# Seven block products in the second product of a mixture of experts, with scatters and searches reordered

## The chip, the cores and the metric

The kernel runs on one core of a Trainium2 chip. The metric is the device time of one execution in microseconds, given as the median over runs; the profile shows one further execution. Engines: PE is TensorE (matmuls; PEld its weight loads), DVE is VectorE, ACT is ScalarE, POOL is GpSimd, SP is the engine that issues most plain DMAs.

## The reference

The program is a stack of four sublayers over tokens of width 256 (4 x 1024 rows): a gated attention, a low-rank feed-forward, a ReLU attention with 16 heads, and a mixture of experts in which each expert chooses its tokens. Each is wrapped as `x = x + layernorm(sublayer(layernorm(x)))`. The change touches only the last one:

```python
def _L1_ffn_ref(x, Wg, W1, b1, W2, b2):
    b, l, h = x.shape                    # 4096 tokens in all, h = 256
    e = Wg.shape[1]                      # 8 experts
    n = b * l
    k = min(max(int(n * 2 / e), 1), n)   # 1024 tokens an expert
    xt = x.reshape(n, h)
    S = jax.nn.sigmoid(xt @ Wg).T
    G, I = jax.lax.top_k(S, k)           # each expert takes its best 1024
    ex = xt[I]
    hid = jax.nn.gelu(jnp.einsum('ekh,ehf->ekf', ex, W1) + b1[:, None, :], approximate=False)   # f = 1024
    out = (jnp.einsum('ekf,efh->ekh', hid, W2) + b2[:, None, :]) * G[..., None]
    new_x = jnp.zeros_like(xt).at[I.reshape(-1)].add(out.reshape(-1, h))
    return new_x.reshape(b, l, h)
```

Everything is float32.

## The kernel before

**The stages.** The first 950 us or so are the three sublayers ahead. From there on the mixture of experts runs, expert after expert. An expert's 1024 chosen tokens are eight chunks of 128; four chunks are a unit, so expert e has the units u = 2e and 2e + 1 (`QPE` is 2, `NJ` is 4 chunks a unit, `TB` is 512 tokens).

**Choosing.** A `Search` (line 1806) finds the 1024th largest score of one or more experts, three bits at a time in ten ticks: VectorE compares and counts, TensorE adds the counts over partitions with one small matmul, VectorE keeps the best candidate. A `List` (line 1891) then turns a threshold into indices: sort, rank, chunks, places, collect, gather. The last step issues eight indirect DMAs on GpSimd's queue that fetch the tokens (`got`). Before the change the searches are for expert 0, for 1, for 2 and 3, and for 4 to 7. Expert 0's search and list run ahead of everything. All other steps stand in one list, `agenda`, and are taken from its head: `go_on_with_lists(u, time)` (line 2357) is called between matmul groups, subtracts `time` from a budget `left`, and runs the next step once the budget is used up and unit u is late enough for it. The first three steps of the second search run while expert 0's tokens are on their way.

**The first product.** `turn` transposes the tokens on TensorE into `xT`. Experts 0, 1, 2 and 7 go through `feed_forward` (line 2275), unit by unit: for each of eight slices f of the hidden width two matmuls with 512 columns, and a gelu on ScalarE into `hid`. Experts 3 to 6 go through `feed_forward_by_seven` (line 2225): both units are handled together as a 2 x 2 block product, with seven block products in place of eight (Strassen's scheme in Winograd's form). The sums of blocks of the weights are made by GpSimd (`weight_sums`), those of the tokens by VectorE (`token_sums`), and the products are combined by VectorE.

**The second product.** `project_back(u, hid)` (line 2307) does one unit. For each of its four chunks, eight matmuls with 256 columns accumulate over the hidden width; VectorE adds the bias and multiplies by the gate; GpSimd issues an indirect DMA that adds the 128 rows to `acc_d` in DRAM (line 2333). The scatters of an expert are ordered among themselves, but for those of expert 6. Between chunks the tokens of the next unit are turned (`turns_within`).

**The last expert.** Expert 7 doesn't scatter. When all scatters of expert 6 have landed (`summed`), `begin_last` reads the accumulator back in blocks of 512 tokens (`read_back`) and fetches expert 7's own rows of it (`fetch_acc`). The table `beside_last` (line 2134) writes out by hand what is done after which matmul group of units 14 and 15: the statistics of a block (`all_stats`, VectorE and GpSimd), its scaling (`all_scaled`, ScalarE), its store (`all_out`), and the same for expert 7's own rows (`chosen_...`).

**What sets the order.** In this stage TensorE, VectorE and ScalarE execute in the order of the program. GpSimd's and SP's order is found by the scheduler, and from expert 6 on GpSimd's too is that of the program. PSUM has five banks tagged `mm` and two tiles tagged `y`.

Of the kernel before, what the change touches and what calls it, by code (L numbers as in the profile page):

```python
# [9 lines left out]
F32 = mybir.dt.float32  # L10
# [4 lines left out]
ALU = mybir.AluOpType  # L15
# [59 lines left out]
def kernel(  # L75
# [1679 lines left out]
    with ExitStack() as st4:  # L1755
# [135 lines left out]
        class List:  # L1891
# [59 lines left out]
            def steps(self):  # L1951

                behind = max(QPE * self.e - 3, 0)
                return [
                    (0.5, behind, self.sort),
                    (2.6, behind, self.rank),
                    (1.2, behind, self.chunks),
                    (1.4, behind, lambda: (self.places(0), self.places(1))),
                    (1.4, behind, lambda: (self.places(2), self.places(3))),
                    (0.3, behind, lambda: [self.collect(part) for part in range(4)]),  # L1960

                    (0.3, behind + 1, self.gather),
                ]
# [62 lines left out]
        summed, stores, replaced, room_back, ys, chosen = [], [], [], [], {}, {}  # L2026
        last = lists[NE - 1]

        def after_all(one, others):
# [90 lines left out]
        def begin_last():  # L2120
# [13 lines left out]
        beside_last = {  # L2134
            (0, "f", 5): [(all_stats, 0)],
            (0, "f", 6): [(all_stats, 1)],
            (0, "f", 7): [(all_scaled, 0), (known, 0), (all_stats, 2), (fetch_acc, 4, 5)],
            (0, "i", 0): [(all_out, 0), (all_scaled, 1), (known, 1), (all_stats, 3)],
            (0, "i", 1): [(all_out, 1), (all_scaled, 2), (known, 2), (all_stats, 4), (fetch_acc, 6, 7)],
            (0, "i", 2): [(all_out, 2), (all_scaled, 3), (known, 3)],  # L2140
            (0, "i", 3): [(all_out, 3), (all_scaled, 4), (all_stats, 5)],
            (1, "f", 0): [(all_out, 4)],
            (1, "f", 1): [(all_scaled, 5, front), (all_stats, 6)],
# [22 lines left out]

        def turn(u, c, half=None):

            if c == 0 and not half:
                xT[u] = wk.tile([P, DC, TB], F32, tag="xT", name="xT")  # L2170
            e, q = divmod(u, QPE)
            tiles = range(NJ) if half is None else range(half * NJ // 2, (half + 1) * NJ // 2)
            tp = ps.tile([P, NJ, P], F32, tag="mm", name="tp", bufs=5)
            for i in tiles:
                nc.tensor.transpose(tp[:, i, :], lists[e].got[q * NJ + i][:, c * P : (c + 1) * P], ident)
                if u == 0 and c == 0 and i == 0:

                    keep_busy(first, 4)
            cols = slice(tiles[0] * P, (tiles[-1] + 1) * P)
            copy = nc.scalar.copy if by_seven(e) else nc.vector.tensor_copy  # L2180
            copy(xT[u][:, c, cols], tp.rearrange("p j t -> p (j t)")[:, cols])  # L2181

        def by_seven(e):

            return 3 <= e < NE - 1

        rooms = [x.rearrange("p j d -> p (j d)")[:, h * TB : (h + 1) * TB] for x in xs[:4] for h in range(2)]
# [21 lines left out]
        def turns_within(u):  # L2209

            e, q = divmod(u, QPE)
            if u == QPE * NE - 1:
                return {}
            turns = {c: (lambda c=c: turn(u + 1, c)) for c in range(DC)}
            if q == QPE - 1 and by_seven(e + 1):
                both = [
                    turns[0], turns[1], lambda: turn(u + 2, 0), lambda: token_sums(e + 1, 0), lambda: turn(u + 2, 1),
                    *(lambda n=n: token_sums(e + 1, n) for n in (1, 2, 3)),
                ]
                return {0: both[0:1], 1: both[1:4], 2: both[4:]}  # L2220
            if by_seven(e) and q == 0:
                return {}
            return {2: [turns[0], turns[1]]} if u == 1 else {1: [turns[0]], 2: [turns[1]]}

        def feed_forward_by_seven(e):
# [14 lines left out]
            def gelu(n, f, src):  # L2240
                gelus.append(nc.scalar.activation(hid[n][:, f, :], src, AF.Gelu, bias=mb1[:, e * FC + f : e * FC + f + 1]))

            HC = FC // 2
            for f in range(HC):
# [20 lines left out]
                nc.vector.tensor_tensor(c12, u2, d, ALU.add)  # L2265
                gelu(1, f, c12)
                go_on_with_lists(QPE * e, 3.0)
            for q in range(QPE):
                if q == 0 and by_seven(e + 1):
                    weight_sums(e + 1, gelus[-1])  # L2270
                if q == 0 and e == NE - 2:
                    fetch_last()
                project_back(QPE * e + q, hid[q])

        def feed_forward(u):
            e, q = divmod(u, QPE)
            w1, w2 = weights[e]
            hid = wk.tile([P, FC, TB], F32, tag="hid", name="hid")

            n = TB if u else TB // 2  # L2280
            for h in range(TB // n):
# [3 lines left out]
                for f in range(FC):  # L2285
# [14 lines left out]
                    if u or h or f not in (FC - 5, FC - 4, FC - 3):  # L2300
                        go_on_with_lists(u, 1.75 if u else 0.87)
                    aside(u, "f", f)
            if q == QPE - 1 and by_seven(e + 1):
                weight_sums(e + 1, gelu)
            project_back(u, hid)

        def project_back(u, hid):
# [4 lines left out]
            for i in range(NJ):  # L2312
                k = q * NJ + i
                py = ps.tile([P, D], F32, tag="y", name="py")
                for f in range(FC):
                    nc.tensor.matmul(  # L2316
                        py,
                        lhsT=hid[:, f, i * P : (i + 1) * P],
                        rhs=w2[:, f, :],
                        start=(f == 0),  # L2320
                        stop=(f == FC - 1),
                    )
                for do in ahead.get(i, ()):
                    do()
                gates = lists[e].got[k][:, D + e : D + e + 1]
                if e == NE - 1:
                    nc.vector.scalar_tensor_tensor(accg[:, k, :], py, gates, accg[:, k, :], ALU.mult, ALU.add)
                    aside(u, "i", i)
                    continue
                y = wk.tile([P, D], F32, tag="y", name="y", bufs=7)  # L2330
                nc.vector.tensor_tensor(y, py, mb2[:, e, :], ALU.add)  # L2331
# [9 lines left out]
                )  # L2341
                if e == NE - 2:

                    beside_each_other(scatter, summed)
                go_on_with_lists(u, 3.4 if by_seven(e) else 2.3)

        searches = [Search(0), Search(1), Search(2, 3), Search(4, 5, 6, 7)]
        agenda = []  # L2350
        for search in searches[1:]:
            agenda.extend(search.steps())
            for e in search.es:
                agenda.extend(lists[e].steps())
        left = [0.0]

        def go_on_with_lists(u, time, within=False):
            left[0] = max(left[0] - time, 0.0)
            if agenda and left[0] < 0.3 and agenda[0][1] <= u and not (within and agenda[0][0] not in (0.5, 1.2, 1.4)):
                spent, _, step = agenda.pop(0)  # L2360
                left[0] += spent
                step()

# [16 lines left out]
        for _ in range(3):  # L2380
            agenda.pop(0)[2]()
            keep_busy(first, 4)
# [51 lines left out]
```

## Time and profile before

| what | us |
| --- | --- |
| median of 3 runs | 1458.32 (1456.48 to 1459.18) |
| the profiled execution, its own time | 1456.37 |
| its span | 1454.2 |
| expert 0, from its first product | 988.68 to 1049.30 |
| expert 1 | 1049.30 to 1108.41 |
| expert 2 | 1108.41 to 1169.19 |
| expert 3 | 1169.19 to 1224.23 |
| expert 4 | 1224.23 to 1279.29 |
| expert 5 | 1279.29 to 1334.33 |
| expert 6 | 1334.33 to 1388.20 |
| expert 7 and the close | 1388.20 to 1454.2 |

The borders of the experts are the starts of their first matmul. In a row of groups the columns are: source line, engine, operation, the tiles that it writes and reads, the shape, the count, then the busy time of the group and the mean duration of one in ns. In a row of the timeline they are: start in us, duration in us of a merged run, engine, line, operation, tiles, count, and in brackets how long the engine stood idle before and what ended that. A row of the table by stage has, for each engine, its busy microseconds and instruction count in that stretch, then the granted TensorE clock (1.00 is full), the busy share of the DMA engines, and GB/s.

### The profile page before, as it was taken

Reading aid. Unit: us, or ns where it says so; the run is one execution under the profiler, and the core shown is the slowest. Engines: PE = TensorE matmul, PEld = TensorE weight load, DVE = VectorE, ACT = ScalarE, POOL = GpSimd, SP = SyncE. Lnnn points to the kernel's source line nnn. Section 1 sums busy time; section 2 is a strip of 40 time slices with the busy share of each in tenths; the row PEclk is TensorE's granted clock in tenths of the full one; section 3 lists DMA queues with packets and bytes.
Section 4 is the critical chain, followed back from the end, with each engine's and each line's share of the span. In section 5 each row is a group of like instructions: output and inputs, shape, how many; then the busy total and the mean of one; then the engine's idle time right before and its main releaser. Section 6 shows DMA issues by size and latency. Waiting matters only on the chain.

```text
span 1454.2 us, 26447 instructions
## 1 busy us (share of the span) xinstructions
PE 1405.7 (97%) x10392; PEld 858.6 (59%) x10392; DVE 869.7 (60%) x2133; ACT 735.8 (51%) x1014; POOL 531.7 (37%) x662
## 2 busy tenths in 40 slices
PE   8999999999889999999999999949999999999997
PEld 4666666666644444454444547727666657757774
DVE  5457555666554637664767496885545766365346
ACT  4244454454358887877787888712122131231243
POOL 4123322322352223422333323413425325543765
PEclk9999999999999999999999999979999999999999
DMA  8400000001652473437344721151414233343364
GB/s 223 142 1 1 0 1 1 1 1 38 203 173 76 122 209 104 143 118 232 91 133 144 229 70 39 39 170 38 106 19 127 51 79 70 78 103 62 81 166 134
DMA packets 104853, 138.76 MB, mean 95 GB/s; under 512 B 25469, under 2 KB 64794, under 8 KB 104602
## 3 DMA queue, kind: packets, MB, share of 16 engines
q1 hardware_dynamic: 74512, 81.75, 18.1%
q0 software_dynamic: 30160, 55.32, 16.1%
q8 instruction: 81, 1.33, 0.4%
q14 instruction: 42, 0.34, 0.1%
q10 hardware_dynamic: 58, 0.01, 0.0%
HBM read 75.29 MB, written 61.51 MB: 94 GB/s over the span
## 4 chain that ended last, share of the span: by engine, by line
PE 87%; DVE 5%; issue 3%; POOL 2%; DMA 1%; ACT 1%; SPq 0%; POOLq 0%; ACTq 0%; DVEq 0%
PE po L1553 16%; PE py L2316 14%; PE sc L1532 10%; PE ph L2290 7%; PE ph L2236 7%; PE pg L722 4%; PE pv L738 4%; PE py L848 3%; PE pt L1308 2%; PE pq L397 2%; PE po L820 2%; PE ph L904 2%; PE pv L431 2%; PE po L824 1%; PE pkv L835 1%
## 5 line engine op out<-in xcount | busy, mean ns | idle before, releaser
L1710 ACT ACTIVATE w<-sc 128x1024 f32<-128x1024 f32 x395 | 379.9, 1023 | 60.7 <-PE sc L1532 60.2
L1553 PE MATMUL po<-w,vaug 128*17 128x256 f32 (+1 forms) x4608 | 256.0, 358 | 1.5 <-DVE turned L1611 1.2
L2316 PE MATMUL py<-w,hid 128*128 128x256 f32 x1024 | 228.6, 380 | 0.0
L2316 PEld LDWEIGHTS py<-w,hid 128*128 128x128 f32 x1024 | 191.9, 190 | 29.6 <-issue 4.2
L1712 DVE TENSOR_SCALAR w<-sc 128x1024 f32<-128x1024 f32 x117 | 142.4, 1220 | 79.4 <-PE sc L1532 75.9
L1553 PEld LDWEIGHTS po<-w,vaug 128*17 128x17 f32 x4608 | 116.3, 97 | 117.9 <-issue 48.2
L1532 PE MATMUL sc<-q,kT 64*128 64x512 f32 (+1 forms) x1152 | 170.3, 403 | 2.5 <-ACT w L1710 1.3
L2333 POOL DMA_INDIRECT acc_d<-y,idx x56 | 88.6, 1583 | 163.0 <-issue 38.6
L1532 PEld LDWEIGHTS sc<-q,kT 64*128 64x128 f32 x1152 | 90.1, 185 | 83.5 <-issue 46.6
L2297 ACT ACTIVATE hid<-ph,mb 128x512 f32<-128x512 f32 (+1 forms) x72 | 46.0, 639 | 159.6 <-PE ph L2290 133.3
L2290 PE MATMUL ph<-xT,w 128*128 128x512 f32 (+1 forms) x288 | 114.8, 552 | 0.3 <-DVE xT L2181 0.3
L2005 POOL DMA_INDIRECT got<-tok_d,idx x64 | 66.6, 1040 | 72.1 <-DVE idx L1995 54.1
L2290 PEld LDWEIGHTS ph<-xT,w 128*128 128x128 f32 x288 | 52.6, 190 | 51.3 <-issue 48.3
L371 POOL DMA_DIRECT2D kT<-k_d x32 | 23.4, 732 | 118.0 <-PE sc L1532 54.0
L722 PE MATMUL pg<-nT,wh 128*128 128x512 f32 x128 | 61.6, 613 | 1.5 <-ACT nT L661 1.5
L2331 DVE TENSOR_TENSOR y<-py,mb 128x256 f32<-128x256 f32 x56 | 23.5, 420 | 64.3 <-PE py L2316 54.9
L848 PE MATMUL py<-wo,oT 128*128 128x256 f32 x256 | 61.6, 384 | 0.0
L738 PE MATMUL pv<-wh,nT 128*128 128x512 f32 x128 | 59.7, 593 | 0.0
L848 PEld LDWEIGHTS py<-wo,oT 128*128 128x128 f32 x256 | 47.5, 190 | 17.6 <-issue 11.1
L746 ACT ACTIVATE v<-v 128x512 f32<-128x512 f32 x32 | 20.2, 630 | 62.7 <-DVE v L745 62.7
L1137 POOL TENSOR_TENSOR rsb<-veb,mhalf 128x1 f32<-128x1 f32 x30 | 19.6, 654 | 86.8 <-DVE veb L1136 86.8
L586 POOL TENSOR_TENSOR x<-x,y 128x1024 f32<-128x1024 f32 x13 | 30.6, 2357 | 56.3 <-ACT y L575 56.3
(352 smaller groups left out, 2344.8 us busy)
## 6 DMA issues: line engine op xcount, KB each, us to landing
q<-q_d POOLq DMA_DIRECT2D x16, 1024.0 KB, 6.0
kT<-k_d POOLq DMA_DIRECT2D x32, 512.0 KB, 8.1
w<-in_L_ffn_W_dram SPq DMA_DIRECT2D x16, 1024.0 KB
k_d<-parts SPq DMA_DIRECT2D x48, 256.0 KB
q_d<-parts SPq DMA_DIRECT2D x48, 256.0 KB
acc_d<-logits SPq DMA_DIRECT2D x8, 512.0 KB
tok_d<-hg SPq DMA_DIRECT2D x30, 128.0 KB
x<-in_L_attn_x_dram SPq DMA_DIRECT2D x7, 512.0 KB
```

What stands on the lines that cost most here:

```text
L722: nc.tensor.matmul(pg, lhsT=wh[:, c, HID + e * P : HID + (e + 1) * P], rhs=d["nT"][:, c, :], start=(c == 0), stop=(c == DC - 1),)
L738: nc.tensor.matmul(pv, lhsT=d["nT"][:, c, i * P : (i + 1) * P], rhs=wh[:, c, 0:HID], start=(c == 0), stop=(c == DC - 1),)
L848: nc.tensor.matmul(py, lhsT=d["oT"][:, e, :], rhs=wo[:, e, :], start=(e == 0), stop=(e == EC - 1))
L1532: nc.tensor.matmul(sc[:, j, m * n : (m + 1) * n], lhsT=row["kT"][t, r][rows, u, (kt + m) * P : (kt + m + 1) * P], rhs=row["q"][qh, t][rows ...
L1553: nc.tensor.matmul(po[rows : rows + HD + 1, at : at + n], lhsT=row["v"][:, kt + m, HQ * t + 4 * r + 2 * u + j, :], rhs=w[:, j, (2 * m + pa ...
L1710: nc.scalar.activation(w, sc, AF.Relu)
L1712: nc.vector.tensor_scalar(w, sc, 0.0, None, ALU.max)
L2005: return nc.gpsimd.indirect_dma_start(out=dst, out_offset=None, in_=rows[:, :], in_offset=self.at_chunk(c), bounds_check=NT - 1, oob_is_er ...
L2236: nc.tensor.matmul(bank, lhsT=a[:, f * P : (f + 1) * P], rhs=b, start=start, stop=stop, skip_group_check=not start)
L2290: nc.tensor.matmul(ph, lhsT=w1[:, c, f * P : (f + 1) * P], rhs=xT[u][:, c, h * n : (h + 1) * n], start=(c == 0), stop=(c == DC - 1),)
L2316: nc.tensor.matmul(py, lhsT=hid[:, f, i * P : (i + 1) * P], rhs=w2[:, f, :], start=(f == 0), stop=(f == FC - 1),)
L2333: scatter = nc.gpsimd.indirect_dma_start(out=acc_d[:, :], out_offset=lists[e].at_chunk(k), in_=y, in_offset=None, bounds_check=NT - 1, oob ...
```

## The change

The second product of experts 1 to 6 is done by a new function, `project_back_by_seven`, for both units of an expert at once. The hidden values are a 2 x 2 block matrix (512 tokens by 512 hidden), W2 is one (512 hidden by 128 columns), and seven block products take the place of eight. A block product is 16 accumulating matmuls of 128 columns. GpSimd makes the sums of W2's blocks (`back_sums`) into the rooms of the attention weights, which are no longer needed; VectorE makes the sums of the hidden blocks, combines the products and adds them, multiplied by the gate, to a tile that ScalarE has filled with bias times gate. All eight scatters of an expert come in two groups: four after the seventh product, four after the last. Experts 1 and 2 keep their first product; their second unit's tokens are now turned within the first unit. Tokens of the experts 1 to 6 are copied out of PSUM by ScalarE, and turned in the `y` banks.

Scatters of one expert are declared independent; each waits for those of the expert before. The searches are for 0, for 1 to 3, and for 4 to 7; the last two have an agenda each, and a step of the second is taken where the head of the first isn't due yet. The sort of a list may begin one unit earlier. Budgets of some calls change, and in the table for the last expert the block statistics come one step later.

```diff
+        def back_sums(e, behind):
+            (b11, b12), (b21, b22) = back_blocks(e)
+            t1, t2, t4 = (room.rearrange("p (f n) -> p f n", n=P) for room in back_rooms[:3])
+            for dst, x, y in ((t1, b12, b11), (t2, b22, t1), (b12, b22, b12), (t4, b21, t2)):
+                after_all(nc.gpsimd.tensor_tensor(dst, x, y, ALU.subtract), [behind])
...
+            def product(bank, a, b, start, stop):
+                for i in range(NJ):
+                    if i == NJ // 2:
+                        lists_too(0)
+                    for f in range(HC):
+                        nc.tensor.matmul(
+                            bank[:, i * P : (i + 1) * P],
+                            lhsT=a[:, f, i * P : (i + 1) * P],
+                            rhs=b[:, f, :],
...
+            def of_bias(q):
+                for k in range(q * NJ, (q + 1) * NJ):
+                    ys[k] = wk.tile([P, D], F32, tag="y", name="y", bufs=9)
+                    nc.scalar.activation(ys[k], mb2[:, e, :], AF.Identity, scale=gates[k])
...
+            p1 = new_bank("p1")
+            product(p1, a11, b11, True, True)
+            nc.scalar.copy(u2, p1)
+            nc.vector.tensor_tensor(s1, a21, a22, plus)
+            nc.vector.tensor_tensor(s3, a11, a21, sub)
+            lists_too(1)
+            p4 = new_bank("p4")
+            product(p4, a22, t4, True, True)
+            nc.vector.tensor_tensor(s2, s1, a11, sub)
+            lists_too(1)
+            product(p1, a12, b21, False, True)
+            of_bias(0)
+            add(0, 0, p1)
+            nc.vector.tensor_tensor(s4, a12, s2, sub)
+            lists_too(1)
+            for do in ahead.get(0, ()):
+                do()
+            p5 = new_bank("p5")
+            product(p5, s1, t1, True, True)
+            nc.scalar.copy(kept, p5)
+            for do in ahead.get(1, ()):
+                do()
+            lists_too(1)
+            p6 = new_bank("p6")
+            product(p6, s2, t2, True, True)
+            nc.vector.tensor_tensor(u2, u2, p6, plus)
+            of_bias(1)
+            for do in ahead.get(2, ()):
+                do()
+            lists_too(1)
+            p7 = new_bank("p7")
+            product(p7, s3, t3, True, True)
+            nc.vector.tensor_tensor(v, u2, p7, plus)
+            nc.vector.tensor_tensor(c21, v, p4, plus)
+            nc.vector.tensor_tensor(v, v, kept, plus)
+            add(1, 0, c21)
+            add(1, 1, v)
+            put(1)
+            lists_too(1)
+            product(p5, s4, b22, False, True)
+            nc.vector.tensor_tensor(u2, u2, p5, plus)
+            add(0, 1, u2)
+            put(0)
...
-        searches = [Search(0), Search(1), Search(2, 3), Search(4, 5, 6, 7)]
-        agenda = []
+        searches = [Search(0), Search(1, 2, 3), Search(4, 5, 6, 7)]
+        agendas = []
...
-            (0, "f", 5): [(all_stats, 0)],
-            (0, "f", 6): [(all_stats, 1)],
-            (0, "f", 7): [(all_scaled, 0), (known, 0), (all_stats, 2), (fetch_acc, 4, 5)],
-            (0, "i", 0): [(all_out, 0), (all_scaled, 1), (known, 1), (all_stats, 3)],
+            (0, "f", 6): [(all_stats, 0)],
+            (0, "f", 7): [(all_stats, 1), (all_scaled, 0), (known, 0), (fetch_acc, 4, 5)],
+            (0, "i", 0): [(all_out, 0), (all_scaled, 1), (known, 1), (all_stats, 2)],
```

`add(q, n, src)` is four gated additions of 128 columns, `put(q)` the four scatters of a unit.

## The prediction

> **What bounds the kernel now.** I read the page's busy row first, then the busy time by stage with cuts at the experts' borders, then the groups by line, then the timeline around single instructions.
>
> ```profile
> PE 1405.7 (97%) x10392; PEld 858.6 (59%) x10392; DVE 869.7 (60%) x2133; ACT 735.8 (51%) x1014; POOL 531.7 (37%) x662
> ```
>
> ```profile
> core 0: us, PE busy (x) PEld busy (x) DVE busy (x) ACT busy (x) POOL busy (x), PEclk, DMA share, GB/s
> 1169.19:1224.23 55.04, 55.04 (x239) 37.48 (x238) 34.15 (x73) 15.26 (x25) 22.57 (x18) 1.00 0.28 70
> 1334.33:1388.20 53.87, 53.87 (x226) 36.16 (x226) 24.31 (x46) 13.16 (x21) 31.97 (x26) 1.00 0.39 82
> 1416.60:1454.20 37.60, 27.73 (x97) 18.05 (x95) 23.63 (x79) 11.04 (x20) 19.89 (x23) 0.93 0.50 133
> ```
>
> In the stages of experts 3 and 6 (first two rows) TensorE is busy all the time at a granted clock of 1.00, and no other engine passes 62%. There a microsecond of TensorE is a microsecond of the kernel. The last row is the close, where TensorE has 10 us of idle time: there the scatters, read-backs and normalization set the end.
>
> **The second product.** It is this group; each float32 matmul is two records, so an expert has 128.
>
> ```profile
> L2316 PE MATMUL py<-w,hid 128*128 128x256 f32 x1024 | 228.6, 380 | 0.0
> L2316 PEld LDWEIGHTS py<-w,hid 128*128 128x128 f32 x1024 | 191.9, 190 | 29.6 <-issue 4.2
> ```
>
> The mean of one is no pace, since neighbours overlap; the timeline gives it, from the start of 16 to the start of what follows:
>
> ```profile
> 1380.85 3.62 PE L2316 MATMUL py<-w,hid 128*128 128x256 f32 x16
> 1384.30 0.60 PE L2175 MATMUL tp<-ident,got 128*128 128x128 f32 x4
> ```
>
> That is 3.45 us for 16, 0.2156 us each, 27.6 us an expert. The change makes seven products of 4 x 4 matmuls of 128 columns: 224 records with 224 loads instead of 128. The nearest row of that shape is early in the kernel:
>
> ```profile
> 79.71 0.38 PE L820 MATMUL po<-packed,v 128*128 128x128 f32 x2
> 79.82 0.30 PEld L824 LDWEIGHTS po<-head,kv 128*128 128x128 f32 x2
> 79.93 0.39 PE L824 MATMUL po<-head,kv 128*128 128x128 f32 x2
> ...
> 81.27 0.39 PE L824 MATMUL po<-head,kv 128*128 128x128 f32 x2
> ```
>
> From 79.71 to 81.27 lie 14 records: 0.1114 us each, a load before every one, the load running beside the matmul in front. So 224 x 0.1114 = 24.95 us, a gain of 2.65 us an expert and **15.9 us** over six. A rule speaks against it: the Trainium skill, "TensorE: Matmul & The Clock Gate", section "The mechanism", says that a weight load overlaps a matmul in flight only when it goes to another row group, and its section "LDWEIGHTS (loading the stationary operand)" puts a load at columns over 1.2, so 107 ns here. Load and matmul in turn would take about 0.218 us, 48.9 us an expert, and six experts would lose 128 us. The row, with full 128-row operands, contradicts the first sentence, and I take the row. The 107 ns still warn that at 0.111 us the loads are close to being the bound.
>
> **Searches.** One search for experts 1 to 3 in place of two (1, then 2 and 3) saves ten ticks; a tick costs TensorE 0.03 us (the tick at 1130.99, the next matmul at 1131.02): **0.3 us**. The first three steps of that search stand in VectorE's queue before the copies of expert 0's first tokens (988.20), and TensorE waits for those. They take 4.2 us now (982.91 to 987.07). With three experts the compare is about 1.0 (four took 1.30) and the reduction 0.86 (0.39, 0.62 and 1.09 for one, two and four), so three compares and two ticks of 0.95 make 7.5 us, to 990.4: **2.2 us lost**. List 1 is ready later: counted by the budgets of the queue its gather is issued at the last hidden slice of unit 1, about 10 us before its tokens are turned, and four gathers with landing need 9 (4 x 1.32 and 2.9 and the index copy): hidden, with 1 us to spare.
>
> **VectorE, ScalarE, GpSimd in the experts.** Per expert VectorE gets four sums of 2048 columns (1.23 us for 1024 in the x sum of L2079, so 2.3 each), five of 512 (0.69), sixteen gated additions of 128 (0.48 for 256, so about 0.35): 18.3 us for the 6.2 us (8 x 0.42 + 0.35) that fall away. Expert 3's stage goes to 46 of 52.4 us: not the bound, but a queue in order. Step by step from the start of the second product (0): s1 is done at 5 and needed by the third new bank at 10.7; s2 at 9 to 12 and needed at 15; s4 at 16 and needed at 23; the last bank is read 1.4 us after the end, and the next expert wants its room 1.7 us after it. All hidden if nothing else blocks VectorE. ScalarE's eight bias scalings (0.59) and two copies (0.58) are 5.9 us in an engine with 40 us idle. The turned tokens only change bank and copier.
>
> GpSimd gets four sums of 512 columns an expert, 5.6 us. They can block VectorE:
>
> ```profile
> 1154.15 4.51 DVE L1824 TENSOR_TENSOR ge<-by_e,tried 128x224 bf16<-128x224 f32 x4
> 1154.21 1.45 POOL L2200 TENSOR_TENSOR x<-w 128x512 f32<-128x512 f32 x1 [9.67 <-ACT hid L2297]
> 1155.74 1.30 POOL L2200 TENSOR_TENSOR w<-w 128x512 f32<-128x512 f32 x1
> ```
>
> Four compares took 4.51 us beside GpSimd's sums, and 1.30 alone. The Trainium skill, "SBUF — State Buffer", section "SBUF: two separate sides", names the cause: a VectorE instruction with two SBUF inputs and a GpSimd one exclude each other for a whole instruction. By the free rows the new sums cost TensorE nothing; by rule and row, expert 1's sums meet the ticks of the search for 4 to 7, which follow each other every 3.5 us with 3.4 us of work, so up to 3.2 us reach TensorE. Bounds 0 and 3.2; I take **2.0**, since list steps may stand there instead. For experts 3 to 6 the operands in the first product lie in PSUM, and the y additions with a PSUM operand ran at 0.42 beside GpSimd: small stalls, 0 to 6 us in all, **0.5** taken, the slack above being longer than one GpSimd sum.
>
> **The close.** Expert 6's eight scatters no longer follow their tiles one by one: four are issued after the seventh product, four after the last. Now:
>
> ```profile
> 1388.19 11.32 PE L2290 MATMUL ph<-xT,w 128*128 128x512 f32 x26
> ...
> 1389.48 1.55 POOL L2333 DMA_INDIRECT acc_d<-y,idx  x1 [1.32 <-DVE y L2332]
> ...
> 1393.42 1.76 SPq L2056 DMA_DIRECT2D back_w<-acc_d  x4
> ...
> 1396.71 1.41 DVE L2046 BATCH_NORM_STATS2 stc<-back_w 128x6 f32<-128x256 f32 x4 [7.50 <-DMA back_w<-acc_d]
> ```
>
> With the end of expert 6 at T = 1388.2, the last scatter starts at T+1.3, the read-backs at T+5.2, the first statistics at T+8.5. After: the seventh product ends at T-3.6, VectorE adds 3 x 0.6 and four tiles of 0.29, and the first y is ready at T. GpSimd spaces scatters by 1.87 us (1370.12, 1372.04, 1373.91), so the eighth starts at T+13.1, the read-backs at T+17.1, the statistics at T+20.4: 11.9 us later against T. Behind the waiting statistics in VectorE's queue stand the additions that free the py banks and the copies of unit 15's tokens; behind the waiting scalings in ScalarE's queue, unit 15's gelus; TensorE waits for both. What absorbs some of it: ScalarE took the first scaling 2.1 us after it could (ready 1400.6, taken 1402.7), and it idles 5.8 us up to the next gelu (1.1 before 1409.82, 2.4 before 1414.26, 2.3 before 1418.60). So between 4.0 and 9.8 us come through. GpSimd's queue keeps the steps in pairs (a store waits for its scaling, the next root stands behind the store), which is nearer the upper end: **8.0**. The shift of the statistics by one step only reorders the wait. The independence of an expert's scatters gains nothing in experts 1 to 5, whose scatters nobody waits for.
>
> **Sum.** -15.9 - 0.3 + 2.2 + 2.0 + 0.5 + 8.0 = -3.5 us. The profiled execution took 1456.37 us (span 1454.2), so 1452.9; the median of the runs is 1.95 above it, so **1454.8 us**.
>
> **Rivals.** (1) The close hides more: the statistics wait, but TensorE's lead in unit 15 and ScalarE's idle time take all but 3 us, and expert 1's ticks miss the sums. -15.9 - 0.3 + 2.2 + 3 = -11: 1447. For it: 10 us of idle TensorE in the last stage; against it: VectorE and ScalarE were nearly full in unit 15. (2) The other side: VectorE's lockout. Expert e+1's GpSimd sums (5.6 us) are queued just where s1, s3 and s2 run, and each 2.3 us sum waits for a 1.3 to 1.8 us one, or scatters delay GpSimd's t4. If that makes an operand late by more than the 2 us of slack in each expert, every further us counts six times; from 0.6 us past it (six times 0.6 is the 3.5 gained) the change no longer pays. At 2 us past it: +12, 1467. Against it: GpSimd is idle for more than half of such a stage (22.6 of 55.0 us busy in expert 3's). (3) The loads do not hide: 1454.8 + 144 = about 1599; the 128-column row speaks against it. (4) List 1 late or the last bank late by 1 to 3 us in two or three experts: 1459.
>
> **Chances.** My forecast 0.55 (its own range 1449 to 1461), rival 1 0.15, rival 2 0.17, rival 3 0.03, rival 4 0.10. 0.2% is 2.9 us, about what the runs can tell from no change. Faster: 0.55 x 0.6 + 0.15 = 0.48. Same: 0.55 x 0.33 + 0.10 x 0.6 + 0.17 x 0.05 = 0.25. Slower: the rest, 0.27. The range for 8 in 10 leaves out rival 3 and the far ends of 1 and 2: 1445 to 1466.
>
> **What would show it.** Each of the stages of experts 4 and 5 at 52.4 us, 224 records at 0.111 us; expert 0's first product 2 us later; a VectorE wait of TensorE in expert 1's second half; the first read-back 17 us after expert 6's last product, and a wait of TensorE for the py bank in unit 14. I am wrong if an expert's stage shrinks by less than 2 us (then the pace or rival 2), or if the time from T to the end grows by less than 4 or more than 10 us from today's 66.0.

## The result and the profile after

The changed kernel takes 1475.81 us (1473.48 to 1476.94, 4 runs), the kernel before 1458.75 (4 runs): a ratio of 1.0113, 95% interval 1.01 to 1.0125. It is slower, by 17 us, where 1454.8 us was forecast. The profiled execution took 1474.76 us, with a span of 1473.0.

The stages, between the first product matmuls of the experts, come from the timelines of both kernels. (Expert 2's border in the table ahead, 1108.41, is where a list's small matmuls start; its first product starts at 1109.36, used here; the other borders there lie up to 0.2 us from these.) The first row runs from the first matmul of a search to expert 0's first product.

| stage | before | after | difference | forecast |
| --- | --- | --- | --- | --- |
| searches and list 0 (from 960.2, from 956.7) | 28.5 | 32.0 | +3.5 | +2.2 |
| expert 0 | 60.5 | 62.8 | +2.3 | 0 |
| expert 1 | 60.2 | 58.1 | -2.1 | -0.9 |
| expert 2 | 59.7 | 57.3 | -2.4 | -2.65 |
| experts 3, 4, 5 | 165.1 | 177.1 | +12.0 | -7.5 |
| expert 6 | 54.0 | 50.05 | -4.0 | -2.65 |
| expert 7 and the close | 66.0 | 79.05 | +13.1 | +8.0 |
| sum | | | +22.4 | -3.5 |

The span grew by 18.8 only, because the three sublayers ahead, which the change leaves alone, happened to take 3.5 us less in this execution. The lists' position matmuls (1.2 us a list) also moved: one list more falls into experts 0 and 2, one less into 1 and 6.

Busy time by stage after, experts 3 to 7; columns as in the same view of before:

```profile
core 0: us, PE busy (x) PEld busy (x) DVE busy (x) ACT busy (x) POOL busy (x), PEclk, DMA share, GB/s
1166.80:1225.48 58.68, 54.52 (x333) 38.77 (x332) 46.19 (x71) 19.75 (x35) 37.28 (x24) 0.97 0.34 73
1225.48:1283.98 58.50, 54.48 (x333) 38.71 (x332) 46.26 (x71) 19.84 (x35) 37.35 (x24) 0.97 0.34 73
1283.98:1343.90 59.92, 55.89 (x334) 39.86 (x332) 46.25 (x71) 19.83 (x35) 37.33 (x24) 0.94 0.32 71
1343.90:1393.95 50.05, 50.05 (x292) 36.55 (x291) 30.19 (x44) 17.34 (x30) 39.50 (x28) 1.00 0.41 86
1393.95:1473.00 79.05, 58.86 (x202) 38.30 (x200) 41.45 (x152) 26.35 (x48) 49.41 (x50) 0.90 0.60 146
```

In expert 6 TensorE is busy all the time. In 3, 4 and 5 it stands idle for 4 us each, and its granted clock falls below 1.00. The waits of TensorE in experts 3 to 5 have one main entry, once in each expert (us in total, times, longest):

```profile
PE ph L2242 <- DVE hid L2259: 10.9, 3, 3.6
PE ph L2242 <- ACT x L2255: 1.3, 3, 0.5
```

That is in the first product, at VectorE's block sums of its third group of slices. Here it is in expert 4, whose first product starts at T = 1225.48 (timeline of after, four stretches):

```profile
1243.25 1.88 DVE L1946 TENSOR_SCALAR pair<-which,in_tile 128x256 bf16<-128x256 bf16 x1
1243.76 1.28 POOL L2294 TENSOR_TENSOR wq<-w 128x512 f32<-128x512 f32 x1
...
1246.39 1.29 POOL L2294 TENSOR_TENSOR wk<-w,wq 128x512 f32<-128x512 f32 x1
...
1246.59 4.68 DVE L1971 TENSOR_TENSOR at<-lo,each 128x1024 bf16<-128x1024 bf16 x2
...
1252.71 2.07 PE L2242 MATMUL ph<-x,w 128*128 128x512 f32 x2 [3.63 <-DVE hid L2259]
```

L2294 is `back_sums`. Its four sums start at T+18 to T+23, while VectorE makes a list's `pair` and `at` (two steps of a `List`). Beside them the pair step takes 1.88 us and the two `at` 4.68. Alone, for list 0 in the kernel before, they take 0.29 and 1.28:

```profile
978.35 0.29 DVE L1946 TENSOR_SCALAR pair<-which,in_tile 128x256 bf16<-128x256 bf16 x1
...
978.88 1.28 DVE L1971 TENSOR_TENSOR at<-lo,each 128x1024 bf16<-128x1024 bf16 x2
```

The block sums queue behind, TensorE stops for 3.63 us, and its next pair of matmuls takes 2.07 us where 1.02 is usual, at a granted clock of 0.50 (1252.70 to 1254.60). The sums come so late because `put` gives GpSimd eight scatters in one block (1226.35 to 1240.98) and two gathers ahead of them; before that block GpSimd had been idle for 15.97 us. In expert 6 the sums come as late (1358.83, T+14.9), but no list is left to be made there, and TensorE doesn't wait.

The close, with T = 1393.93 (timeline of after):

```profile
1393.93 13.90 PE L2421 MATMUL ph<-xT,w 128*128 128x512 f32 x32
...
1396.44 1.62 POOL L2346 DMA_INDIRECT acc_d<-y,idx  x1 [5.25 <-DVE y L2342]
...
1409.51 1.56 POOL L2346 DMA_INDIRECT acc_d<-y,idx  x1 [0.31 <-issue]
...
1413.46 1.76 SPq L2057 DMA_DIRECT2D back_w<-acc_d  x4
...
1416.89 1.41 DVE L2047 BATCH_NORM_STATS2 stc<-back_w 128x6 f32<-128x256 f32 x4 [18.67 <-DMA back_w<-acc_d]
...
1422.41 5.67 PE L2454 MATMUL py<-w,hid 128*128 128x256 f32 x16 [7.24 <-DVE accg L2467]
```

The read-backs start at T+19.5 (before: T+5.2) and the statistics at T+23.0. TensorE waits 7.24 us for a `py` bank and then runs 16 matmuls in 5.67 us, not 3.62; the granted clock is 0.50 up to 1424.40 and 0.73 from there to 1428.10.

### The profile page after: what moved, and what is told of

Its sections match the earlier page's. It is cut to its first block, busy times and chain, and to the rows that moved or that the text cites. A ratio compares the mean times of both kernels' runs of the same rounds, so it can differ in the third digit from the quotient of the medians.

```text
span 1473.0 us, 27769 instructions
## 1 busy us (share of the span) xinstructions
PE 1399.6 (95%) x10958; PEld 867.5 (59%) x10958; DVE 947.1 (64%) x2140; ACT 766.2 (52%) x1082; POOL 593.0 (40%) x685
## 4 chain that ended last, share of the span: by engine, by line
PE 82%; DVE 9%; DMA 3%; issue 3%; POOL 2%; ACT 1%; SPq 0%; POOLq 0%; DVEq 0%; ACTq 0%
PE po L1553 15%; PE p L2324 10%; PE sc L1532 10%; PE ph L2421 6%; PE ph L2242 5%; PE pg L722 4%; PE pv L738 4%; PE py L848 3%; PE pt L1308 2%; PE py L2454 2%; PE pq L397 2%; PE po L820 2%; PE ph L904 2%; PE pv L431 2%; PE po L824 1%
## 5 line engine op out<-in xcount | busy, mean ns | idle before, releaser
L2346 POOL DMA_INDIRECT acc_d<-y,idx x48 | 75.1, 1564 | 119.4 <-DVE y L2342 107.9
L2005 POOL DMA_INDIRECT got<-tok_d,idx x64 | 72.2, 1129 | 55.6 <-DVE idx L1995 38.0
L2324 PEld LDWEIGHTS p<-w,hid 128*128 128x128 f32 x768 | 89.4, 195 | 4.8 <-issue 4.8
L2324 PE MATMUL p<-w,hid 128*128 128x128 f32 x768 | 90.4, 278 | 0.0
L2454 PE MATMUL py<-w,hid 128*128 128x256 f32 x256 | 60.3, 392 | 8.7 <-DVE accg L2467 7.2
L738 PE MATMUL pv<-wh,nT 128*128 128x512 f32 x128 | 59.7, 592 | 0.0
L2454 PEld LDWEIGHTS py<-w,hid 128*128 128x128 f32 x256 | 48.9, 196 | 18.1 <-DVE accg L2467 7.5
```

The lines of the kernel that those rows point to most:

```text
L738: nc.tensor.matmul(pv, lhsT=d["nT"][:, c, i * P : (i + 1) * P], rhs=wh[:, c, 0:HID], start=(c == 0), stop=(c == DC - 1),)
L2324: nc.tensor.matmul(bank[:, i * P : (i + 1) * P], lhsT=a[:, f, i * P : (i + 1) * P], rhs=b[:, f, :], start=start and not i and not f, stop= ...
L2346: scatter = nc.gpsimd.indirect_dma_start(out=acc_d[:, :], out_offset=lists[e].at_chunk(k), in_=ys[k], in_offset=None, bounds_check=NT - 1, ...
L2454: nc.tensor.matmul(py, lhsT=hid[:, f, i * P : (i + 1) * P], rhs=w2[:, f, :], start=(f == 0), stop=(f == FC - 1),)
```

## The experiments

The theories: **A**, `back_sums` holds up VectorE in experts 3 to 5, and expert 6's bunched scatters lengthen the close. **B**, VectorE simply has too much to do, or the block of scatters and gathers slows it; the close is longer because of the shifted table. Kernels of one session share runs of the kernel before, whose median was 1461.15, 1454.58, 1459.68, 1454.93 and 1454.56 us in the five sessions (runs 1 to 4, 5 to 8, 9 to 12, 13 and 14, 15 and 16). So ratios are the measure, and stages.

### 1. Sums early

```diff
             product(p6, s2, t2, True, True)
+            back_sums(e + 1, <its last matmul>)
...
-                if f == 0:
-                    back_sums(e, gelus[-1])
```

> The changed kernel, but the four GpSimd sums of a second product's weights (back_sums) of experts 2 to 6 are issued half a product to two products earlier: right behind the last matmul of product p6 of the expert before, ahead of that expert's eight scatters, where GpSimd stands idle for some 16 us. Expert 1's stay where they are. Theory A (the two-tensor sums of GpSimd lock VectorE out[...] just where it makes a list's pair and `at`, so that the block sums of the first product's third group come late): experts 3, 4 and 5, now 58.7, 58.5 and 59.9 us, come to 52.4 to 54 us each, the close stays at 79, and the time falls by 15 to 20 us, to about 1457. Rival B (VectorE has too much to do in these experts wherever the sums stand, or it is the scatters and gathers on GpSimd that slow it): the three experts stay within 2 us of their times and the time falls by less than 5 us, to 1471 or more. Rival C (the sums do the same harm at the new place, to the sums behind p7): between the two, 1460 to 1471, with TensorE waiting at p7 or at the last product.

Measured: 1459.75 us, ratio 0.9994 (0.9984 to 1.0004). The stages from expert 3 on:

```profile
1171.09:1224.38 53.29, 52.54 (x334) 38.17 (x333) 43.71 (x70) 19.74 (x35) 38.33 (x24) 1.00 0.36 81
1224.38:1277.65 53.27, 52.54 (x334) 38.18 (x332) 43.62 (x70) 19.74 (x35) 38.32 (x24) 1.00 0.37 80
1277.65:1330.93 53.28, 52.54 (x333) 38.18 (x332) 43.64 (x70) 19.74 (x35) 38.34 (x24) 1.00 0.36 80
...
1381.99:1460.10 78.11, 59.09 (x202) 37.95 (x200) 39.69 (x147) 26.34 (x48) 47.95 (x50) 0.93 0.60 148
```

Experts 3 to 5 lose 17.3 us against the changed kernel, by moving four GpSimd instructions. Theory A holds; B would have left them. The close hardly changes (78.1). Some 0.8 us an expert remain: at the new place the sums meet the token sums (1.75 us in place of 0.69), behind which the sums after p7 wait. From the first search matmul this kernel still takes 499.3 us against the 493.9 of before; why its ratio is nevertheless near 1 is told with the stall of runs 13 to 16.

### 6. Sums left out

The sums for experts 3 to 6 are not made at all:

```diff
-                if f == 0:
-                    back_sums(e, gelus[-1])
```

> The changed kernel without the GpSimd sums of the second product's weights for experts 3 to 6: four sums an expert are left out, so these experts' second products use sums of an earlier expert and a right-hand block that was not subtracted; everything else, scatters, gathers and list steps included, stands where it was. Theory A (the sums' hold on VectorE is the whole loss in experts 3 to 5): these stages fall from 58.5 to 59.9 us to 52.4 to 53.2 us each, the first step of a list's pair takes about 0.3 us instead of 1.9 and the two at steps 2.6 us instead of 4.7; the time falls by 17 to 20 us against the changed kernel. Rival B (the list steps or the bunched scatters and gathers on GpSimd make the stall): the stages stay at 57 us or more.

Measured: 1455.07 us, ratio 1.0007 (0.9997 to 1.0017). Experts 3 to 5:

```profile
1167.94:1220.41 52.47, 52.47 (x333) 38.23 (x332) 41.42 (x71) 19.72 (x35) 32.01 (x20) 1.00 0.36 82
1220.41:1272.83 52.42, 52.42 (x334) 38.24 (x332) 41.35 (x71) 19.65 (x35) 31.93 (x20) 1.00 0.36 82
1272.83:1325.25 52.42, 52.42 (x334) 38.23 (x332) 41.37 (x71) 19.67 (x35) 31.97 (x20) 1.00 0.36 81
```

52.42 us is the forecast 52.4, with scatters, gathers and list steps where they were. In the second of them:

```profile
1238.12 0.52 DVE L1946 TENSOR_SCALAR pair<-which,in_tile 128x256 bf16<-128x256 bf16 x1
...
1239.85 1.28 DVE L1971 TENSOR_TENSOR at<-lo,each 128x1024 bf16<-128x1024 bf16 x2
```

Against the changed kernel expert 4 loses its 4.0 us of idle time and 2.1 us of TensorE's busy time, which are the wait and the slower matmuls behind it. So the sums' hold on VectorE is the whole loss in these experts, and the forecast pace of the seven products is right.

### 2, 3 and 5. The close

Run 2 puts expert 6's second product back; run 3 means to delay its scatters in the kernel before, and run 5 does so:

```diff
# 2
-            return 1 <= e < NE - 1
+            return 1 <= e < NE - 2
# 3: the scatters of all eight y behind the last chunk; 5: the same, and
+                        after_all(scatter, [last_scaled_y])
```

> The changed kernel with expert 6's second product as the kernel before has it: eight plain chunks, each with its scatter as soon as it is done. Theory A (the close is 13 us longer because expert 6's eight scatters are all issued behind its last products): the close falls from 79 to 66 to 69 us, expert 6's stage rises by 2.65 to about 52.7 us, and the time falls by 8 to 11 us, to 1465 to 1468. Rival B (the close is longer because of the shifted table of side steps and what it makes GpSimd wait for): the close stays above 75 us and the time doesn't fall, 1474 to 1478.

> The kernel before with one thing changed: expert 6 holds its eight scatters back and issues all of them behind its last chunk (nine buffers of y instead of seven). Its products and the table of side steps are as before. Theory A (late scatters alone make the close long): the close rises from 66 by 9 to 13 us and the time to 1468 to 1472. Rival B (the table, the order of the two halves, or the late v of the changed kernel makes most of it): the close rises by less than 5 us, and the time stays under 1464.

> The kernel before with one thing changed: none of expert 6's eight scatters may start before the last chunk's y is scaled (in the run before this one they were only issued last, and each still left as soon as its own y was there, so that it delayed nothing). Products and the table of side steps are as before. Theory A (late scatters make the close long): the first scatter starts some 2 us after the close's first matmul, the read-backs some 18 to 20 us after it, the close takes 74 to 78 us instead of 66, and the time rises by 8 to 11 us, that is by 0.5 to 0.8 per cent. Rival B (late scatters are hidden by expert 7's first product, or only the table of side steps matters): the close stays under 70 us.

Run 3 tested nothing of this: on GpSimd the eight scatters already followed each other, each waiting for its own y only, so they left as before and the close stayed at 65.97 us (ratio 0.9994). Run 2's close and run 5's:

```profile
1404.14:1473.20 69.06, 56.67 (x201) 36.91 (x199) 37.98 (x140) 26.24 (x48) 36.66 (x43) 0.95 0.59 156
```

```profile
1387.88:1472.40 84.52, 62.41 (x201) 40.68 (x199) 37.56 (x140) 26.84 (x48) 49.94 (x50) 0.87 0.57 137
```

In run 2 the close falls by 10.0 us, as A says. The time does not follow: 1475.17 us, ratio 1.0100 (1.008 to 1.0121), since expert 6 takes 56.8 us and not 52.7 (the stall again). In run 5 late scatters alone, with the table of before, add 18.6 us to the close in the profiled execution. That one is the slowest of four (1464.72 to 1474.68 us); between the medians it is 14.6 us (1469.13 against 1454.58), still more than expected; ratio 1.0096 (1.0075 to 1.0116). The start of this is as reckoned, the rest is not:

```profile
1389.18 1.62 POOL L2340 DMA_INDIRECT acc_d<-y,idx  x1 [19.67 <-DVE y L2334]
...
1406.23 2.40 SPq L2056 DMA_DIRECT2D back_w<-acc_d  x4
...
1417.79 6.40 PE L2318 MATMUL py<-w,hid 128*128 128x256 f32 x16 [8.66 <-DVE accg L2329]
...
1447.79 1.22 PE L2318 MATMUL py<-w,hid 128*128 128x256 f32 x2 [3.38 <-ACT hid L2297]
```

The read-backs are at T+18.4. TensorE waits 8.66 us, then needs 2.8 us more for 16 matmuls (granted clock 0.50, then 0.59), and from the last second product on (1441.65 to the end) it takes 30.75 us, 6.9 more than before: all steps of the table are late, and it stalls a second time.

### 4. The searches alone

```diff
-        searches = [Search(0), Search(1), Search(2, 3), Search(4, 5, 6, 7)]
+        searches = [Search(0), Search(1, 2, 3), Search(4, 5, 6, 7)]
```

and two agendas, due times and ticks as in the change, in the kernel before.

> The kernel before with only the list part of the change: one search for experts 1 to 3 and one for 4 to 7, two queues of steps, the new due times and ticks; every second product is plain. Forecast as the prediction had it: expert 0 longer by 2.1 us, experts 1 to 6 as before, so +2 us, 1460 to 1461. Rival: one search less and its due times also take stalls out of experts 1 and 2 (59.1 and 60.8 us in the kernel before against 55.0 for 3 to 5), so that it is faster by 1 to 5 us, 1453 to 1457.

Measured: 1463.68 us, ratio 1.0023 (1.0014 to 1.0031), 2.5 us more between the medians. Ahead of expert 0 lie 31.8 us instead of 28.5, in it 64.3 instead of 60.5; experts 1 to 5 give back 0.9. From the index copy of list 0 to the first copy of tokens it takes 9.0 us, before 5.7. Not all of these 3.3 us are the three steps: run 7, with the same steps, takes 7.8, so that they cost 2.1, and 2.2 was counted. The rest goes with TensorE's clock. In this stretch TensorE runs matmuls that only keep it busy, and the tokens are turned behind some of them; the granted clock was 1.00 before and in run 7, but 0.81 here and 0.70 in the changed kernel (9.2 us). Why it falls in some runs is open. The stages sum to 6.3 us more than those of before; the time shows less because most executions of the kernel before that ran beside it seem to hold the stall of runs 13 to 16.

### 7. and 12. Early sums, expert 6 plain, old table

> The changed kernel with three parts put differently: the sums early as in the first run, expert 6's second product plain as in the second, and the table of side steps of the kernel before. Theory A: experts 3 to 5 take 53.3 us each as in the first run; the close is 66 us, 3 us less than with the shifted table (69.1 in the second run), since the last chunks of expert 7 no longer wait for statistics one row later; expert 6 takes 53 us, or up to 57 if TensorE stalls there again for y as it did in three runs; 1450 to 1455 us where the kernel before takes 1461 on this chip, a ratio of 0.993 to 0.996. Rival: the table makes no difference and the close stays at 69 us: 1453 to 1458.

Measured: 1447.50 us, ratio 0.996 (0.9947 to 0.9974); run again as the neighbour of runs 9 to 11, 0.9964 (0.995 to 0.9977). This is faster than both kernels.

> The seventh run's kernel once more, as the neighbour of the three runs ahead on the same chip: a ratio of 0.995 to 0.997 to the kernel before, stages as in the seventh run, within 0.3 us but for the start, whose length has varied by 1.4 us between runs.

The close of run 7:

```profile
1377.53:1443.50 65.97, 56.13 (x201) 37.07 (x199) 38.06 (x140) 26.57 (x48) 37.48 (x43) 0.96 0.61 163
```

3.1 us less than run 2's: beside early scatters, that is the shift of the table by one step. So of the close's 13.1 us about 10 go when expert 6's scatters are early, and 3 more with the table of before. The place fits: in the changed kernel 9.4 us come ahead of the first product of unit 15 and 3.6 after it starts; run 2 has nothing ahead of it and 3.1 after. But the two can't simply be added: in run 5, with late scatters and the table of before, the part after it grows by 7.0. The changed kernel with the table of before was not run.

### 8. Seven products for experts 3 to 5 alone

> The kernel before with nothing of the change but the second products of experts 3, 4 and 5 in seven block products (their sums early: expert 3's beside expert 2's first product, the others' behind p6 of the expert before), scatters independent and nine y buffers; searches, due times, table and the second products of experts 1, 2 and 6 are as before. Theory A: experts 3 to 5 take 53.3 us instead of 55.0, three times 1.7 is 5 us, nothing else moves: a ratio of 0.995 to 0.998. Rival: the single queue of list steps finds too few ticks within the seven products, a list comes late and TensorE waits for its gather: a ratio over 1.000.

Measured: 1459.32 us, ratio 1.0036 (1.0022 to 1.005). Experts 4 and 5 take 54.3 us, but expert 2 takes 62.1 instead of 59.7, expert 3 takes 56.8, and the close 67.8. In expert 2, where expert 3's sums had been put, TensorE waits for the compare of a search tick:

```profile
1142.61 3.36 DVE L1824 TENSOR_TENSOR ge<-by_e,tried 128x224 bf16<-128x224 f32 x4
```

```profile
1147.14 0.18 PE L1838 MATMUL parts<-counts,all_b 128*128 128x32 bf16 x1 [2.35 <-DVE counts L1831]
```

I expected nothing to move there and made the same error again: the sums beside VectorE's list work. In expert 3 the rival came true: the gathers of expert 4's tokens begin only at 1196.67, TensorE waits twice for them, 1.26 and 0.96 us (1212.73 and 1214.02), and the 32 matmuls behind take 5.08 us and not 3.74. What lengthens the close by 1.8 us was not traced.

### 9, 10 and 11. The start, expert 1's sums, halves

```diff
# 9: two search steps ahead of expert 0's tokens, not three
-        for _ in range(3):
-            agendas[0].pop(0)[2]()
+        for n in range(3):
+            if n < 2:
+                agendas[0].pop(0)[2]()
# 10
-                    if e == 1 and q and not f:
+                    if e == 1 and not q and f == FC - 1:
                         back_sums(e, gelu)
# 11: both, and two sums behind p5, two behind p6
+            back_sums(e + 1, <last matmul of p5>, 0)
...
+            back_sums(e + 1, <last matmul of p6>, 2)
```

> The seventh run's kernel (sums early, expert 6's second product plain, the table of before) with two steps of the search for experts 1 to 3 ahead of expert 0's tokens in place of three; the third step is taken later, from the queue. Theory A (these steps hold up the copies of expert 0's first tokens): from the index copy of list 0 to the first copy of tokens it takes 5.7 us, as in the kernel before, where the seventh run had 7.8 and the changed kernel 9.2; 2 to 3 us less in the profiled span from the first search matmul, provided list 1 still comes in time. Rival: list 1 is one tick later and TensorE waits for its tokens at the start of expert 1, so nothing is won.

> The seventh run's kernel with expert 1's four sums on GpSimd issued behind the last gelu of expert 1's first unit in place of the first gelu of its second: some 2 us earlier, where VectorE stands idle and GpSimd's gathers have ended. Theory A (the sums make the second tick of the search for experts 4 to 7 late): TensorE's wait of 1.7 us for the counts in expert 1 goes, and expert 1's stage falls from 58.1 to about 56.4 us. Rival: the wait stays, because VectorE's tick is late for another reason.

> The seventh run's kernel with both of these edits, and with the sums of experts 2 to 6 in two halves: two behind product p5's last matmul, two behind p6's. Theory A: 2 to 3 us at the start, 1.7 us in expert 1, and experts 3 to 5 fall from 53.3 to 52.4 to 52.9 us each, since VectorE's token sums then meet two sums of GpSimd and not four: 5 to 7 us less than the seventh run's kernel beside it, 1439 to 1444 on a chip where the kernel before takes 1455. Rival: the first two sums now meet VectorE's s4 or the sum behind p6 and TensorE waits there: experts 3 to 5 stay at 53.3 us or rise.

Beside run 12 (1454.41 us): run 9 1451.16, run 10 1452.41, run 11 1448.56 us; ratios 0.9943, 0.9946 and 0.9925 (0.9911 to 0.9938). Run 11 is the fastest of the four. All four have the stall of the next section in expert 6, whose stage takes 58.0, 56.6 and 58.3 us in runs 9, 10 and 11 and 59.3 in run 12, so that small differences of the totals mean little; run 10's 2.0 us are no more than that. In run 9 it takes 7.6 us from list 0's index copy to the first copy of tokens, and in run 12 8.9; the granted clock is 0.55 and 0.81. In run 11, with run 9's start and a clock of 1.00, it takes 5.4. But the rival of run 9 came true as well: list 1 is later, and TensorE waits 2.0 us for its tokens (2.1 in run 11). In run 10 the wait for the counts in expert 1 falls from 1.7 to 0.2 us and the stage from 58.1 to 56.6. In run 11 experts 3 to 5 fall from 53.3 to 52.8, 52.5 and 52.5.

### 13 to 16. A stall in expert 6, left open

In the first and third session every profile with a plain second product of expert 6 (runs 2, 3, 4, 9 to 12) has a stall in it: the stage takes 56 to 60.6 us (60.6 in run 3, which in effect is the kernel before). In runs 5, 7 and 8 it takes 54.1, 52.7 and 54.8. The stall as run 12 shows it, VectorE first, then TensorE:

```profile
1369.72 0.42 DVE L2477 TENSOR_TENSOR y<-py,mb 128x256 f32<-128x256 f32 x1 [7.66 <-remote]
```

```profile
1370.20 9.98 PE L2460 MATMUL py<-w,hid 128*128 128x256 f32 x32 [3.59 <-DVE y L2477]
```

Runs 13 and 14 issue each gather of expert 7's own rows just ahead of a scatter of expert 6, in run 11's kernel and in the one before; 15 and 16 are runs 11 and 13 again, side by side.

> The eleventh run's kernel with the eight gathers of expert 7's own rows (xg) issued one ahead of each scatter of expert 6, where they stood as one block of eight ahead of all of them. Theory A (VectorE's and then TensorE's stall in expert 6 comes with an unbroken train of indirect DMAs on GpSimd, at whose end TensorE's late signals arrive): the train ends with the list's gathers, expert 6's stage falls from 56.5 to 59.3 us to 52.7, as it was in the seventh run, and no wait for a remote event is left in its chunks; 4 to 6 us less than the eleventh run, a ratio of 0.988 to 0.991. Rival B (the stall has nothing to do with the train, it comes and goes by itself): expert 6 keeps 56 us or more, ratio 0.992.

> The kernel before with the same single edit: one gather of xg ahead of each scatter of expert 6. Theory A: expert 6's stage is 54.0 us as in the profile of before (which had no stall), and the median falls by 1 to 4 us, because the stall that the third and fourth run's profiles showed in this stage is then gone from all executions: a ratio of 0.997 to 0.999. Rival B: no difference, 1.000.

> The eleventh run's kernel once more, beside the next one on the same chip. Theory A (the stall belongs to some chips or sessions, those in which the kernel before takes 1459 us and more, and comes with the block of gathers): if the kernel before takes 1459 us or more here, expert 6's stage is 56 to 60 us; if it takes about 1455 us, 52.7 us.

> The thirteenth run's kernel (gathers between the scatters) once more. Theory A: expert 6's stage is 52.7 us whatever the kernel before takes here; where that is 1459 us or more this kernel is 4 to 6 us faster than its neighbour, the eleventh run's. Rival B (the train of gathers has nothing to do with it): it stalls as its neighbour does, both 56 us or more, or both 52.7.

Ratios: run 13 0.993 (0.9916 to 0.9943), run 14 1.0000 (0.9992 to 1.0009), run 15 0.9927 (0.991 to 0.9943), run 16 0.9932 (0.9916 to 0.9949). Expert 6 takes 52.65 us in 13, 15 and 16 and 54.0 in 14. But run 15, with the block of gathers unbroken, has no stall either: it was absent from these two sessions, so whether the train of gathers makes it stays open. It goes with the session, and not with the chip (the first and the fourth session had the same one), and with a kernel before that takes 1459 us or more. A kernel whose expert 6 isn't plain escapes most of it (51.1 us in run 1). So run 1 comes out level with a kernel before of 1461, although its stages sum to 5 us more than the profile of before, which has no stall: run 3, of the same session, takes 500.4 us from the first search matmul, run 1 499.3.

## Why the prediction was wrong

**The pace was right.** 32 records of 128 columns take 3.57 us (1368.05 to 1371.62), 0.1116 each against 0.1114 forecast, with a load before every one:

```profile
1368.05 3.73 PE L2324 MATMUL p<-w,hid 128*128 128x128 f32 x32
1371.62 3.74 PE L2324 MATMUL p<-wv,hid 128*128 128x128 f32 x32
```

Run 6 shows the promised gain (2.65 us forecast, 2.6 measured) in three experts, unobstructed: 52.42 against 55.04. The rule of the Trainium skill that a load overlaps only with a matmul on other row groups ("TensorE: Matmul & The Clock Gate", "The mechanism") would have made these stages longer; the row decided rightly.

**The step that failed** is the one on VectorE in experts 3 to 6: "small stalls, 0 to 6 us in all, 0.5 taken, the slack above being longer than one GpSimd sum". Experts 3 to 5 lost 19.5 us against the forecast, over three times the upper bound. The rule of the Trainium skill, "SBUF — State Buffer", section "SBUF: two separate sides", was in hand, with its row (four compares 4.51 us beside GpSimd's sums, 1.30 alone), but I applied it to expert 1 only, and looked in experts 3 to 6 at the wrong VectorE instructions: at the block sums, whose operand lies in PSUM, and at s1 to s4. The list steps, `pair` and `at`, which stand in the same queue ahead of the block sums, I left out (the pair step has one tensor input only, and was stretched all the same), and I did not work out when GpSimd would get to the sums. From the numbers at hand it follows: eight scatters at 1.87 us put the sums 15 us and more after the expert's start, into the list steps. The trace agrees with the rule: in expert 4 three GpSimd sums run from 1246.39 to 1250.11, 3.7 us, and the two `at` beside them lose 3.4.

**Rival 2** had the mechanism and the side, and its 1467 was the nearest of the times. Its place was wrong: the weight sums did slow s1, s3 and s2 (3.2 to 3.4 us in place of 2.28 in experts 3 to 5), but that stayed hidden; the harm was in the next expert's first product.

**The close** was 8.0 with bounds of 4.0 to 9.8 and measured 13.1. The mechanism was right, and the wait that it forecast is the 7.24 us of TensorE. The read-back was nearly right: T+19.5 for T+17.1. The sum behind p7 started 1.8 us later than forecast (1392.14), after a wait that the trace calls remote, as in the stall of runs 13 to 16. Two terms were missing. "The shift of the statistics by one step only reorders the wait" is wrong beside early scatters, where it costs 3.1 us (run 2 against run 7), and in the changed kernel expert 7's second half grew by 3.6. And after its wait of 7.24 us TensorE ran the next 16 matmuls 2.1 us slower, at the lower granted clock. The bounds counted only what ScalarE could absorb.

**The start** was 2.2 and measured 3.5, in run 4 3.3. The steps were counted rightly (2.1 in run 7, at a full clock); what was missing is the lower granted clock of that stretch, 0.70. That expert 0 itself grows by 2.3 us (one list more, 1.2, the rest not traced) was not foreseen. List 1 came in time, as forecast: in expert 0 TensorE doesn't wait for its tokens. **Expert 1's ticks** were right: 2.0 forecast, 1.70 measured as a wait for counts at 1076.33, and run 10 removes 1.5 of it. Expert 6's extra 1.3 us is the list that moved out of it.

## What to carry to other kernels

When work goes to GpSimd, find the time at which its queue gets to it, and look at what VectorE has there, the small bookkeeping steps included; GpSimd's two-input sums stretched VectorE's small list steps and compares here by 2.6 to 6.5 times (3.36 us for 1.30, 1.88 for 0.29), and the instructions queued behind paid for it. A block of scatters delays everything behind it in the queue as much as it delays what waits for the data. And an unfavourable result need not condemn the idea: with the four sums in the idle time ahead of the scatters, and expert 6 and the table left alone, the same seven products make the kernel 0.4% faster than before, with three more moves (run 11) 0.75%.

## What the runs showed of the hardware

- One GpSimd sum of 128 x 512 float32 takes 1.28 us alone, 3.2 us beside a VectorE sum of 128 x 2048, which itself takes 3.2 to 3.4 instead of 2.28 (up to 3.8 in run 1). Bfloat16 list steps suffer more: 0.29 to 1.88 us, and 1.28 to 4.68 for two.
- After 3.6 us of waiting TensorE ran a pair of matmuls in 2.07 us instead of 1.02 at a granted clock of 0.50, after 8.7 us sixteen in 6.40 instead of 3.62 at 0.50 and 0.59 (run 5): these stalls cost their length and 1 to 3 us more. After the 2.35 us of run 8 the clock stayed at 1.00, and the next eight took their usual 3.68.
- With the same steps ahead of expert 0, TensorE was granted a clock of 1.00 in one run and less in another (1.00 in run 11, 0.55 in run 9; 1.00 in run 7, 0.81 in run 12); from list 0's index copy to the first copy of tokens the runs of lower clock took 2.2 and 1.0 us more.
- In some sessions VectorE waits up to 9.0 us (run 3; 7.7 in run 12) for a signal that the trace calls remote, although TensorE's records show the matmuls finished long before. The kernel before differs by up to 6.6 us between sessions, probably for this reason in the main (run 3 spends 6.6 us more in expert 6 than the profile of before); only kernels run side by side should be compared.
